# Adaptive-LayerNorm block: the opening's modulation and projections cut by 256 features instead of 512

## The chip, the cores and the metric

The kernel runs on one core of a Trainium2 chip. The metric is the device time of one execution in microseconds (us), taken as the median of several runs. TensorE is called PE in the profile (PEld is its weight load), VectorE DVE, ScalarE ACT, GpSimd POOL, and SyncE, which only issues DMAs here, SP.

## What is computed

The input is x, 2048 tokens of 1024 features, in float32. A conditioning vector c gives six rows of 1024 values, and two sublayers use three rows each:

```python
mod = (silu(c) @ wmod).reshape(1, 6, 1, 1024)        # sa, ca, ga, sb, cb, gb
h = layernorm(x) * (1 + ca) + sa
x = x + ga * attention(h, Wq, Wk, Wv, Wo)            # ga, gb: magnitude at least 0.25
h = layernorm(x) * (1 + cb) + sb
x = x + gb * lora_experts(h, route_w, A, Bw)         # one of 8 experts of rank 16
```

The attention is causal, with 32 query heads and 8 key heads of width 32, and rotates queries and keys by position (cos and sin tables) before the scores.

## The kernel before, in words

The work is one static program: every engine has its queue of instructions in a fixed order, and waits on semaphores. The order has two parts. The function `open_up` (L1334) writes out by hand the *opening*, the projections of token block 0 (256 tokens). From there on, a planner (`plan_order`, L97) searches an order of attention, the other blocks' projections, the output product and the second sublayer; it keeps a list of the eight PSUM banks by the time at which it believes each to be free (`gates`, L1649 to 1655: times on entry are constants), and gives each piece of work the first of them. Its first pieces after the opening are the four flips and the values of block 1, called `second`.

Weights and tokens come through two streams (`Stream`, L579). A stream has a list of wanted loads, taken in order, and `pump` issues as many as there are free buffers: five of 512 KB for weights ("w"), four for tokens ("x"). `free` gives buffers back and pumps again. All these DMAs are issued by SP in program order, so a load whose buffer is still being read holds up what stands behind it on SP. Blocks 0 and 1 share weights that stay on the chip ("resident"): values and keys in `vk` tiles, queries in `wq` tiles.

A `Modulation` item (L762) makes 512 columns of one row of `mod`. It takes four weight tiles, multiplies them with silu(c) (tile `mr`, L790), copies the result to `rows` on DVE (L796), then turns it into columns, one value per partition (tile `mc`, L802), and writes them to `mod_cols[i]` on DVE (L808, L810). Row 1 is the scale, row 0 the shift of the first sublayer. Four items precede everything else, in the order scale, shift (features 0 to 511), scale, shift (features 512 to 1023).

The tokens of a block are normalised in place (L690 to 733, DVE and ACT). A *flip* (`feature_major`, L746) transposes 128 tokens by 512 features on PE into one PSUM bank (`tr_a`, L751) and writes them to `h_t` with scale and shift, four operations of 128 columns: on ACT for the first half of the features (L738), on DVE for the second (L742). `h_t` has eight chunks of 128 features, and each product goes over the chunks: 2 x 8 for values, 2 x 8 for keys (both L684), 4 x 2 x 8 for queries (L975), each of four matmuls on a quarter of the array's columns.

In the opening six banks are held open as sums (0: values, 1: keys, 2 to 5: queries), and banks 6 and 7 alternate for everything else. The order on PE is: items one and two, flips of features 0 to 511, values and keys for these, item three, two query banks, item four, the third query bank, flips of features 512 to 1023, the fourth query bank, then values, keys and the four query banks for the second half. The norm of the second block (`second.pre()`) is issued after the second flips.

Sums leave PSUM at the end: values by a copy on ACT (`keep_values`, L956), keys and queries by `rotary` (L843). It multiplies by cos on DVE into `tcos` (L849), swaps half heads on DVE into `swap` (L850), and on POOL multiplies `swap` by sin (L853) and adds (L854):

```python
tcos = two.tile([P, 2, TB], F32, tag="half", name=f"tcos_{name}", bufs=3)
swap = two.tile([P, 2, TB], F32, tag="half", name=f"swap_{name}", bufs=3)
```

The tag "half" has three buffers, taken in turn by all that use it. The PSUM bank is free after the swap.

Of the kernel before, what the change touches and what calls it, by code (L numbers as in the profile page):

```python
# [10 lines left out]
F32 = mybir.dt.float32  # L11
# [6 lines left out]
P = 128  # L18
T = 2048
D = 1024  # L20
# [5 lines left out]
QB = 512  # L26
NQB = T // QB
TB = 256
# [444 lines left out]
def adaln_block_kernel(  # L473
# [24 lines left out]
    nc = tc.nc  # L498
# [80 lines left out]
    class Stream:  # L579
        def __init__(self, pool, tag, depth):  # L580
            self.pool, self.tag, self.depth = pool, tag, depth
            self.loads, self.tiles = [], []
            self.freed = self.used = 0

        def pump(self, most=1 << 30):
            while len(self.tiles) < min(len(self.loads), self.freed + self.depth, most):
                n = len(self.tiles)
                shape, load = self.loads[n]
                t = self.pool.tile(shape, F32, tag=self.tag, name=f"{self.tag}_{n}")
                load(t)  # L590
                self.tiles.append(t)
# [14 lines left out]
    weights = Stream(wpool, "w", NW)  # L606
    tokens = Stream(xpool, "x", NX)

    def want_wmod(i, half):
        for kp in range(NC // 2):  # L610
            col = i * D + half * 512
            src = wmod[kp * 2 * P : (kp + 1) * 2 * P, col : col + 512].rearrange(
                "(k p) n -> p k n", p=P
            )
            weights.loads.append(([P, 2, 512], lambda t, s=src: nc.sync.dma_start(t, s)))

    resident = {}

    def load_values_keys(kh):

        rows = slice(kh * 512, (kh + 1) * 512)
        t = epool.tile([P, 4, QB], F32, tag="et", name=f"vk_{kh}")
        for i, w in enumerate((wv, wk)):
            nc.sync.dma_start(
                t[:, :, i * TB : (i + 1) * TB], w[rows, :].rearrange("(k p) n -> p k n", p=P)
            )
        resident["vk", kh] = t

    def load_queries(kh, half):
        for kp in (2 * kh, 2 * kh + 1):  # L630
            t = qpool.tile([P, 2, QB], F32, tag="q", name=f"wq_{half}_{kp}")
            nc.sync.dma_start(
                t,
                wq[kp * 2 * P : (kp + 1) * 2 * P, half * 512 : (half + 1) * 512].rearrange(
                    "(k p) n -> p k n", p=P
                ),
            )
            resident["q", half, kp] = t

# [122 lines left out]
    class Modulation:  # L762
# [1 line left out]

        when = -1

        def __init__(self, i, half):
            self.i, self.half = i, half

        def plan(self, push):  # L770
            slow = 0.2 if self.i in mod_cols else 2.4
            return [
                Part(1.7, "C", True, (("dve", 0.7),), chunks=4, push=push),
                Part(0.9, "W", True, (("dve", slow),), frees=4),
            ]

        def want(self):
            want_wmod(self.i, self.half)

        def pre(self):  # L780
            return []

        def main(self, following):
            i, half = self.i, self.half
            parts = weights.take(4)
            ps = bank(f"mr_{i}_{half}")
            for r in range(2):
                for q in range(4):
                    k = r * 4 + q
                    nc.tensor.matmul(  # L790
                        ps[q * HD : (q + 1) * HD, :], silu_p[:, k, :], parts[k // 2][:, k % 2, :],
                        start=(r == 0), stop=(r == 1),
                    )
                weights.free(2)
            rows = two.tile([P, 512], F32, tag="half", bufs=3, name=f"rows_{i}_{half}")
            nc.vector.tensor_copy(rows, ps)  # L796
            following()
            yield 1.7, True
            ps = bank(f"mc_{i}_{half}")
            if i in mod_cols:  # L800
                for j in range(4):
                    nc.tensor.matmul(  # L802
                        ps[:, j : j + 1], rows[:, j * P : (j + 1) * P], ones_p[:, 0:1],
                        start=True, stop=True,
                    )
                dst = mod_cols[i][:, half * 4 : half * 4 + 4]
                if i in (1, 4):
                    nc.vector.tensor_scalar_add(dst, ps[:, 0:4], 1.0)  # L808
                else:
                    nc.vector.tensor_copy(dst, ps[:, 0:4])  # L810
            else:


                nc.tensor.matmul(ps, ones_p, rows, start=True, stop=True)
                cols = slice(half * 512, (half + 1) * 512)
                sgn = two.tile([P, 512], F32, tag="half", bufs=3, name=f"gsgn_{i}_{half}")
# [23 lines left out]
    def sign_rotation(cs):  # L840
        nc.scalar.activation(cs[:, 1, :], cs[:, 1, :], AF.Identity, scale=sign)
# [14 lines left out]
    class Project:  # L856
# [80 lines left out]
        def flip(self, s, kh):  # L937
            feature_major(
                self.h_t[:, :, s * P : (s + 1) * P], self.xt[s], kh, mod_cols[1], mod_cols[0],
                f"a_{self.b}_{s}_{kh}",  # L940
            )

        def first(self, part, k):

# [344 lines left out]
    m = {(i, half): Modulation(i, half) for i in (2, 3, 4, 5) for half in range(2)}  # L1289
# [35 lines left out]
    def fill(n=1):  # L1325
        for _ in range(n + 4):
            step = advance()
            assert step is not None
            n -= bool(step[0])
            if not n:  # L1330
                return step[0]
        raise AssertionError("the next part of an item cannot be issued yet")

    def open_up():  # L1334


# [6 lines left out]
        load_values_keys(0)  # L1343
        load_queries(0, 0)
        fill(2)
        opening.start()
        for s in range(2):
            opening.flip(s, 0)
        chosen[:0] = range(6)
        banks = [bank("open") for i in range(6)]  # L1350

        def values(kh):
            for s in range(2):
                for k in range(4 * kh, 4 * kh + 4):
                    opening.value(banks[0], s, k)

        def keys(kh):
            for a in range(2):
                for k in range(4 * kh, 4 * kh + 4):
                    opening.key(banks[1], a, k)  # L1360

        def queries(kh, i):
            for a in range(2):
                for k in range(4 * kh, 4 * kh + 4):
                    opening.query(banks[2 + i], i // 2, 2 * (i % 2) + a, k)

        values(0)
        keys(0)
        load_queries(0, 1)
        fill(2)  # L1370
        load_values_keys(1)
        for half in range(2):
            load_queries(1, half)
        tokens.pump()
        cs = load_rotation(0, 2)
        for i in range(4):
            opening.query_tiles(i // 2, i % 2)
        queries(0, 0)
        queries(0, 1)
        fill(2)  # L1380
        queries(0, 2)
        for s in range(2):
            opening.flip(s, 1)
            tokens.free()
        sign_rotation(cs)
        for _, act in second.pre():
            act()
        queries(0, 3)
        values(1)
        keys(1)  # L1390
        opening.keep_values(banks[0])
        opening.keep_keys(banks[1])
        for half in range(2):
            for hp in range(2):
                queries(1, 2 * half + hp)
            for hp in range(2):
                opening.keep_queries(banks[2 + 2 * half + hp], half, hp)
        chosen.clear()


# [352 lines left out]
```

## Time and profile before

| | us |
|---|---|
| median of three runs (1755.1 to 1756.59) | 1755.84 |
| the profiled execution | 1754.85 |
| its span, first to last instruction | 1752.6 |
| first matmul | 8.51 |
| first product of the opening | 21.70 |
| end of the opening, first transposes of block 1 | 72.63 |
| first values of block 1 | 74.53 |

The mean granted clock of TensorE is 0.998 of full speed. Over the first 62 us the DMA engines are busy without a break, at 350 to 410 GB/s. In lines of the timeline the first number is the start and the second the length in us, then come engine, line of the kernel, operation and tiles (output<-input); brackets hold the idle time before it and what ended it. Lines of the chain of waits hold start, length and what the chain passed through. Names of tiles are the program's, with buffer numbers left out.

### The profile page before, as it was taken

The numbers are of one execution on the slowest core, as the hardware profiler recorded it, in microseconds if no ns is written. First come the engines' busy times: TensorE is split into PE (matmuls) and PEld (weight loads), VectorE is DVE, ScalarE is ACT, GpSimd is POOL, SyncE is SP. The second block draws the span as 40 slices with busy tenths as digits, with TensorE's granted clock in tenths as the row PEclk, the third lists the DMA queues.
The fourth block names the chain that finished last, engine by engine and source line by source line (L and its number), as shares of the span: only waits on it lengthen the run. The fifth ranks groups of instructions, "written<-read, shape, count | busy, mean of one in ns | idle before, by whom it ended". The sixth has DMA issues, their size and how long they took to land.

```text
span 1752.6 us, 55165 instructions
## 1 busy us (share of the span) xinstructions
PE 1716.0 (98%) x24616; PEld 704.6 (40%) x24616; DVE 1089.0 (62%) x2160; ACT 737.9 (42%) x1634; POOL 1297.5 (74%) x630
## 2 busy tenths in 40 slices
PE   7999999999999999999999999999999999999997
PEld 3655554444444433334444443323323333333334
DVE  2455556756656764675667545756675675776487
ACT  2203423443543433445435444244444544454463
POOL 1235646578878775869786989789889899898952
PEclk9999999999999999999999999999999999999999
DMA  9502323212322512222013011110111111101001
GB/s 354 185 27 83 115 81 104 64 60 98 104 65 65 180 72 82 73 79 68 24 59 128 26 50 49 68 44 36 50 55 46 48 50 50 73 26 50 34 5 50
DMA packets 68493, 130.52 MB, mean 74 GB/s; under 512 B 3744, under 2 KB 20768, under 8 KB 68256
## 3 DMA queue, kind: packets, MB, share of 16 engines
q1 hardware_dynamic: 66928, 125.85, 20.7%
q8 instruction: 193, 3.16, 0.7%
q10 hardware_dynamic: 1328, 1.15, 0.2%
q14 instruction: 44, 0.36, 0.1%
HBM read 118.59 MB, written 8.39 MB: 72 GB/s over the span
## 4 chain that ended last, share of the span: by engine, by line
PE 77%; POOL 15%; DVE 2%; issue 2%; ACT 1%; DMA 1%; SPq 0%; POOLq 0%; ACTq 0%; DVEq 0%
POOL acc L1571 14%; PE sm L1445 13%; PE po L1553 12%; PE sc L1535 11%; PE pq L975 11%; PE pw L684 10%; PE sc L1521 4%; PE pk L684 3%; PE pv L684 2%; PE pd L1580 2%; PE open L975 2%; PE mr L790 1%; PE pf L684 1%; DVE mx L1452 1%; PE pa L684 1%
## 5 line engine op out<-in xcount | busy, mean ns | idle before, releaser
L1452 DVE TENSOR_REDUCE mx<-sm 128x1 f32<-128x512 f32 (+3 forms) x1280 | 686.7, 601 | 400.7 <-PE sm L1445 399.8
L1571 POOL TENSOR_TENSOR acc<-acc,et 128x2048 f32<-128x2048 f32 (+1 forms) x242 | 905.1, 3740 | 28.1 <-ACT et L1543 14.8
L1543 ACT ACTIVATE et<-sc 128x512 f32<-128x512 f32 (+3 forms) x1280 | 575.5, 543 | 662.4 <-PE sc L1535 645.1
L1445 PE MATMUL sm<-k_t,q 32*128 32x512 f32 (+3 forms) x3328 | 335.3, 475 | 3.0 <-ACT rd L1585 3.0
L1553 PE MATMUL po<-et,v_sb 128*32 128x512 f32 (+3 forms) x2560 | 296.6, 539 | 0.6 <-ACT et L1543 0.5
L1535 PE MATMUL sc<-q,k_t 32*128 32x512 f32 (+3 forms) x2560 | 291.0, 533 | 0.0
L684 PE MATMUL pw<-w,q 128*32 128x512 f32 x1920 | 235.5, 597 | 1.4 <-DMA w<-in_wo_dram 1.4
L1445 PEld LDWEIGHTS sm<-k_t,q 32*128 32x128 f32 x3328 | 139.0, 185 | 131.0 <-issue 48.6
L975 PE MATMUL pq<-h_t,w 128*32 128x256 f32 x3072 | 187.9, 382 | 0.0
L1569 POOL TENSOR_TENSOR acc<-et,et 128x2048 f32<-128x2048 f32 (+1 forms) x31 | 132.1, 4262 | 38.6 <-ACT et L1543 24.9
L975 PEld LDWEIGHTS pq<-h_t,w 128*32 128x32 f32 x3072 | 90.6, 110 | 103.8 <-issue 48.7
L1121 POOL TENSOR_TENSOR x<-ag,x 128x512 f32<-128x512 f32 x40 | 64.4, 1611 | 90.2 <-DVE ag L1120 81.5
L1553 PEld LDWEIGHTS po<-et,v_sb 128*32 128x32 f32 x2560 | 61.7, 109 | 166.9 <-issue 137.7
L1535 PEld LDWEIGHTS sc<-q,k_t 32*128 32x128 f32 x2560 | 119.0, 185 | 14.1 <-issue 2.8
L1589 DVE RECIPROCAL rd<-rd 128x128 f32<-128x128 f32 x128 | 113.6, 922 | 17.0 <-ACT rd L1585 16.8
L1521 PE MATMUL sc<-nt,ones_h 32*128 32x512 bf16 (+3 forms) x1280 | 115.2, 351 | 1.8 <-DVE mx L1452 1.0
L1521 PEld LDWEIGHTS <-ones_h 32*128 32x128 bf16 x1280 | 31.2, 91 | 196.7 <-issue 186.9
L684 PEld LDWEIGHTS pw<-w,q 128*32 128x32 f32 x1920 | 51.4, 109 | 139.5 <-issue 116.9
L853 POOL TENSOR_TENSOR swap_q<-swap_q,cs 128x512 f32<-128x512 f32 x32 | 40.7, 1273 | 60.9 <-DVE swap_q L850 60.8
L853 POOL TENSOR_TENSOR swap_k<-swap_k,cs 128x512 f32<-128x512 f32 x8 | 10.2, 1277 | 94.7 <-DVE swap_k L850 94.7
L1120 DVE TENSOR_TENSOR ag<-pw,gate 128x512 f32<-128x512 f32 x40 | 27.5, 686 | 63.4 <-PE pw L684 61.5
L1593 POOL TENSOR_TENSOR q<-q,rd 128x512 f32<-128x512 f32 x31 | 39.6, 1277 | 35.4 <-DVE rd L1589 28.8
(146 smaller groups left out, 1278.4 us busy)
## 6 DMA issues: line engine op xcount, KB each, us to landing
w<-in_wo_dram SPq DMA_DIRECT2D x112, 256.0 KB
w<-in_wmod_dram SPq DMA_DIRECT2D x48, 512.0 KB
w<-in_wq_dram SPq DMA_DIRECT2D x48, 512.0 KB
x<-in_x_dram SPq DMA_DIRECT2D x32, 512.0 KB
out_dram<-x SPq DMA_DIRECT2D x16, 512.0 KB
w<-in_wv_dram SPq DMA_DIRECT2D x12, 512.0 KB
w<-in_wk_dram SPq DMA_DIRECT2D x12, 512.0 KB
wq<-in_wq_dram SPq DMA_DIRECT2D x8, 512.0 KB
```

Source lines behind the costliest of these rows:

```text
L684: nc.tensor.matmul(dst[rows], left[:, rows], right, start=start, stop=stop)
L975: nc.tensor.matmul(ps[j * HD : (j + 1) * HD, a * TB : (a + 1) * TB], self.query_weights(half, k, j * P + h * HD), self.h_t[:, k, :], start ...
L1121: nc.gpsimd.tensor_add(x1[t][:, cols], tmp, x1[t][:, cols])
L1445: nc.tensor.matmul(ps[j][:, a:b], q[rows, t * P : (t + 1) * P], k[rows, kc * QB + o : kc * QB + o + b - a], start=not masked, stop=(t, a, ...
L1452: nc.vector.tensor_reduce(mx[:, t, j : j + 1, kc], ps[j][:, a:b], AX.X, ALU.max)
L1521: nc.tensor.matmul(ps[j][:, a:b], ones_h[rows, :], nt[rows, off:], start=(kc == kcs[0]), stop=False,)
L1535: nc.tensor.matmul(ps[j][:, a:b], k[rows, kc * P : (kc + 1) * P], q[rows, off:], start=False, stop=(kc == kcs[-1]),)
L1543: nc.scalar.activation(self.ets[kc][:, j, off:], ps[j][:, a:b], AF.Exp, scale=1.0 / math.sqrt(HD))
L1553: nc.tensor.matmul(self.po[rows, off:], v_sb[:, kc, 4 * (self.m // 4) + j, :], et[:, j, off:], start=(i == 0), stop=(i == self.nk - 1),)
L1569: self.adder.tensor_add(self.acc[:, :, off:], first[:, :, off:], et[:, :, off:])
L1571: self.adder.tensor_add(self.acc[:, :, off:], self.acc[:, :, off:], et[:, :, off:])
L1589: nc.vector.reciprocal(part, part)
```

## The change

An item of the opening now makes scale and shift of the *same* 256 features, so that after each item two chunks of `h_t` can be made and multiplied. Its four weight tiles are each filled by two DMAs of 256 columns. `flip_chunks` transposes two chunks of both token tiles into one bank and applies scale and shift by two operations of 256 columns, both on ACT. The resident weights are loaded by 256 rows: one call of `load_resident` issues four DMAs (values, keys, two halves of queries). `Stream.pump` keeps its limit, so that SP's order of wmod and resident weights is set by `weights.most`.

The opening is a loop over four steps of 256 features: values, keys, three query banks, half of the fourth, the next item's rows, the other half, the item's columns, the next flips. The last step has no item and keeps each sum as it is done. The norm of the second block comes after the last flips, ahead of the last step. The planner, its constants and what follows the opening are as before.

```diff
@@ Stream @@
-        def pump(self, most=1 << 30):
-            while len(self.tiles) < min(len(self.loads), self.freed + self.depth, most):
+            self.most = 1 << 30
+        def pump(self, most=None):
+            self.most = most or self.most
+            while len(self.tiles) < min(len(self.loads), self.freed + self.depth, self.most):
@@ wanted loads @@
-    def want_wmod(i, half):
...
+    def want_wmod(pieces):
         for kp in range(NC // 2):
+            def load(t, kp=kp):
+                at = 0
+                for i, col, n in pieces:
+                    nc.sync.dma_start(
+                        t[:, :, at : at + n],
+                        wmod[kp * 2 * P : (kp + 1) * 2 * P, i * D + col : i * D + col + n].rearrange(
+                            "(k p) n -> p k n", p=P
+                        ),
+                    )
+                    at += n
+            weights.loads.append(([P, 2, 512], load))
-    def load_values_keys(kh):
-    def load_queries(kh, half):
...
+    def load_resident(kp):
+        rows = slice(kp * 2 * P, (kp + 1) * 2 * P)
+        kh, at = kp // 2, kp % 2 * 2
+        if kp % 2 == 0:
+            resident["vk", kh] = epool.tile([P, 4, QB], F32, tag="et", name=f"vk_{kh}")
         for i, w in enumerate((wv, wk)):
             nc.sync.dma_start(
+                resident["vk", kh][:, at : at + 2, i * TB : (i + 1) * TB],
+                w[rows, :].rearrange("(k p) n -> p k n", p=P),
             )
+        for half in range(2):
             t = qpool.tile([P, 2, QB], F32, tag="q", name=f"wq_{half}_{kp}")
             nc.sync.dma_start(
+                t, wq[rows, half * 512 : (half + 1) * 512].rearrange("(k p) n -> p k n", p=P)
             )
             resident["q", half, kp] = t
@@ Modulation.main @@
+                at = 0
+                for i, col, n in self.pieces:
+                    dst, n = mod_cols[i][:, col // P : (col + n) // P], n // P
+                    if i in (1, 4):
+                        nc.vector.tensor_scalar_add(dst, ps[:, at : at + n], 1.0)
+                    else:
+                        nc.vector.tensor_copy(dst, ps[:, at : at + n])
+                    at += n
@@ Project @@
+        def flip_chunks(self, k0):
+            ps = bank(f"tr_a_{self.b}_{k0}")
+            for i in range(2):
+                for s in range(2):
+                    nc.tensor.transpose(
+                        ps[:, (2 * i + s) * P : (2 * i + s + 1) * P],
+                        self.xt[s][:, (k0 + i) * P : (k0 + i + 1) * P], ident,
+                    )
+            for i in range(2):
+                modulate(
+                    self.h_t[:, k0 + i, :], ps[:, i * TB : (i + 1) * TB],
+                    mod_cols[1], mod_cols[0], k0 + i, True,
+                )
@@ items @@
-    start_items = [Modulation(i, half) for half in range(2) for i in (1, 0)]
+    start_items = [Modulation((1, col, TB), (0, col, TB)) for col in range(0, D, TB)]
@@ open_up @@
         tokens.pump(2)
-        weights.pump()
+        weights.pump(4)
+        load_resident(0)
+        weights.most = 8
         chosen.extend([6, 7] * 8)
         for _, act in opening.pre():
             act()
         fill(2)
...
+        load_resident(1)
         opening.start()
...
+        opening.flip_chunks(0)
         chosen[:0] = range(6)
         banks = [bank("open") for i in range(6)]
...
+        def queries(kp, i, parts=range(2)):
+            for a in parts:
+                for k in (2 * kp, 2 * kp + 1):
+                    opening.query(banks[2 + i], i // 2, 2 * (i % 2) + a, k)
+        for kp in range(4):
+            for s in range(2):
+                for k in (2 * kp, 2 * kp + 1):
+                    opening.value(banks[0], s, k)
+            for a in range(2):
+                for k in (2 * kp, 2 * kp + 1):
+                    opening.key(banks[1], a, k)
+            if kp == 3:
+                opening.keep_values(banks[0])
+                opening.keep_keys(banks[1])
+                for i in range(4):
+                    queries(kp, i)
+                    if i % 2:
+                        for hp in range(2):
+                            opening.keep_queries(banks[1 + i + hp], i // 2, hp)
+                break
+            for i in range(3):
+                queries(kp, i)
+            weights.most = 12 + 4 * kp if kp < 2 else 1 << 30
+            queries(kp, 3, [0])
+            fill(1)
+            if kp == 0:
+                load_resident(2)
+            elif kp == 1:
+                load_resident(3)
+                cs = load_rotation(0, 2)
+                tokens.pump(1 << 30)
+            queries(kp, 3, [1])
+            fill(1)
+            opening.flip_chunks(2 * kp + 2)
+            if kp == 2:
+                tokens.free(2)
+                sign_rotation(cs)
+                for _, act in second.pre():
+                    act()
         chosen.clear()
```

More of the change, by code (lines that the diff above doesn't have):

```diff
@@ L607, in adaln_block_kernel @@
     tokens = Stream(xpool, "x", NX)
-    def want_wmod(i, half):
+    def want_wmod(pieces):
         for kp in range(NC // 2):
[L611 to L615, printed above, removed]
-    resident = {}
-    def load_values_keys(kh):
-        rows = slice(kh * 512, (kh + 1) * 512)
-        t = epool.tile([P, 4, QB], F32, tag="et", name=f"vk_{kh}")
+            def load(t, kp=kp):
[9 more added lines that the diff above has]
+            weights.loads.append(([P, 2, 512], load))
+    resident = {}
+    def load_resident(kp):
[3 more added lines that the diff above has]
+            resident["vk", kh] = epool.tile([P, 4, QB], F32, tag="et", name=f"vk_{kh}")
         for i, w in enumerate((wv, wk)):
             nc.sync.dma_start(
-                t[:, :, i * TB : (i + 1) * TB], w[rows, :].rearrange("(k p) n -> p k n", p=P)
-            )
-        resident["vk", kh] = t
-    def load_queries(kh, half):
-        for kp in (2 * kh, 2 * kh + 1):
+                resident["vk", kh][:, at : at + 2, i * TB : (i + 1) * TB],
+                w[rows, :].rearrange("(k p) n -> p k n", p=P),
+            )
+        for half in range(2):
             t = qpool.tile([P, 2, QB], F32, tag="q", name=f"wq_{half}_{kp}")
             nc.sync.dma_start(
[L633 to L636, printed above, removed]
+                t, wq[rows, half * 512 : (half + 1) * 512].rearrange("(k p) n -> p k n", p=P)
             )
@@ L765, in adaln_block_kernel, with __init__ @@
         when = -1
-        def __init__(self, i, half):
-            self.i, self.half = i, half
+        def __init__(self, *pieces):
+            self.pieces = pieces
         def plan(self, push):
-            slow = 0.2 if self.i in mod_cols else 2.4
+            slow = 0.2 if self.pieces[0][0] in mod_cols else 2.4
             return [
@@ L777, in want @@
         def want(self):
-            want_wmod(self.i, self.half)
+            want_wmod(self.pieces)
         def pre(self):
@@ L783, in main @@
         def main(self, following):
-            i, half = self.i, self.half
+            i, col, _ = self.pieces[0]
             parts = weights.take(4)
-            ps = bank(f"mr_{i}_{half}")
+            ps = bank(f"mr_{i}_{col}")
             for r in range(2):
@@ L794, in main @@
                 weights.free(2)
-            rows = two.tile([P, 512], F32, tag="half", bufs=3, name=f"rows_{i}_{half}")
+            rows = two.tile([P, 512], F32, tag="half", bufs=3, name=f"rows_{i}_{col}")
             nc.vector.tensor_copy(rows, ps)
@@ L798, in main @@
             yield 1.7, True
-            ps = bank(f"mc_{i}_{half}")
+            ps = bank(f"mc_{i}_{col}")
             if i in mod_cols:
@@ L805, in main @@
                     )
[L806 to L810, printed above, removed]
+                at = 0
[6 more added lines that the diff above has]
+                    at += n
             else:
                 nc.tensor.matmul(ps, ones_p, rows, start=True, stop=True)
-                cols = slice(half * 512, (half + 1) * 512)
-                sgn = two.tile([P, 512], F32, tag="half", bufs=3, name=f"gsgn_{i}_{half}")
+                cols = slice(col, col + 512)
+                sgn = two.tile([P, 512], F32, tag="half", bufs=3, name=f"gsgn_{i}_{col}")
                 nc.vector.tensor_scalar(sgn, ps, 0.0, 0.5, ALU.is_ge, ALU.subtract)
@@ L1286, in adaln_block_kernel @@
     opening, second = Project(0), Project(1)
-    start_items = [Modulation(i, half) for half in range(2) for i in (1, 0)]
+    start_items = [Modulation((1, col, TB), (0, col, TB)) for col in range(0, D, TB)]
     early, late = outputs(0)
-    m = {(i, half): Modulation(i, half) for i in (2, 3, 4, 5) for half in range(2)}
+    m = {(i, half): Modulation((i, half * 512, 512)) for i in (2, 3, 4, 5) for half in range(2)}
     phases = [
@@ L1342, in open_up @@
         fill(2)
-        load_values_keys(0)
-        load_queries(0, 0)
-        fill(2)
+        load_resident(1)
         opening.start()
-        for s in range(2):
-            opening.flip(s, 0)
+        opening.flip_chunks(0)
         chosen[:0] = range(6)
         banks = [bank("open") for i in range(6)]
[L1352 to L1375, printed above, removed]
         for i in range(4):
             opening.query_tiles(i // 2, i % 2)
-        queries(0, 0)
@@ L1379, in open_up @@
[L1379 to L1397, printed above, removed]
+        def queries(kp, i, parts=range(2)):
+            for a in parts:
+                for k in (2 * kp, 2 * kp + 1):
+                    opening.query(banks[2 + i], i // 2, 2 * (i % 2) + a, k)
```

## The prediction, on record before the changed kernel ran

> **What bounds the kernel now.** I read the page first, then the chain of waits in order of time over the first 90 us, the timeline of VectorE at the end of the opening, and a table of stretches for DMA rates and the granted clock. The page says that TensorE sets the time:
>
> ```profile
> PE 1716.0 (98%) x24616; PEld 704.6 (40%) x24616; DVE 1089.0 (62%) x2160; ACT 737.9 (42%) x1634; POOL 1297.5 (74%) x630
> ...
> PE 77%; POOL 15%; DVE 2%; issue 2%; ACT 1%; DMA 1%; SPq 0%; POOLq 0%; ACTq 0%; DVEq 0%
> ```
>
> Nothing past the opening is edited. The question is how much sooner or later TensorE comes through the opening and into the second block. The chain there (start, length, what):
>
> ```profile
> 8.51 5.50 PE mr L790 x16
> ...
> 14.04 0.70 DVE rows L796
> ...
> 14.88 1.02 PE mc L802 x8
> ...
> 21.70 7.11 PE open L684 x128
> ...
> 33.13 7.04 PE open L975 x128
> 40.17 1.79 PE mr L790 x16
> ...
> 41.98 0.70 DVE rows L796
> ...
> 42.72 1.05 PE mc L802 x8
> ...
> 72.70 1.90 PE tr_a L751 x16
> 74.60 7.04 PE pv L684 x128
> ```
>
> The chain runs on TensorE from 8.5 us to beyond 88 us, apart from DVE's copies of 0.7 us, so a delay here is paid at the end in full. The products begin at 21.70, the opening ends at 72.63, the second block's values begin at 74.53. The next view is VectorE at that border:
>
> ```profile
> 58.95 0.69 DVE L849 TENSOR_TENSOR tcos_k<-open,cs 128x512 f32<-128x512 f32 x1 [3.33 <-PE open L684]
> ...
> 59.57 0.74 DVE L850 STREAM_SHUFFLE swap_k<-open 128x512 f32<-128x512 f32 x1
> ...
> 66.74 0.01 DVE L850 LOAD_MASK_SELECT swap_q<-open  x1 [0.19 <-POOL q L854]
> ...
> 73.73 0.73 DVE L850 STREAM_SHUFFLE swap_q<-open 128x512 f32<-128x512 f32 x1
> 74.36 2.63 DVE L742 TENSOR_SCALAR h_t<-tr_a,mod,mod 128x128 f32<-128x128 f32 x8
> ```
>
> Five rotations (keys, four query banks) stand one behind the other. From the third on, a shuffle waits for POOL: three "half" buffers serve them, so each shuffle needs the buffer that the rotation before it gives back after its POOL addition. The shuffles start 3.50 us apart (66.74, 70.24, 73.73). Before, that costs nothing, because TensorE finishes a query bank every 3.5 us too. Behind the last shuffle in DVE's queue stand the second block's transposed features (L742), needed at 74.53 + 4 x 0.43 = 76.26, when the values reach feature chunk 4. They come 1.5 us early.
>
> **The change, part by part.**
>
> *The start.* One item instead of two precedes the products. Its four loads now have rows of 1 KB, where they had 2 KB:
>
> ```profile
> 8.00:12.50 4.50, 3.99 (x14) 0.73 (x16) 3.95 (x13) 0.81 (x4) 1.59 (x4) 1.00 1.05 402
> ...
> 36.50:39.50 3.00, 3.00 (x61) 1.82 (x56) 0.00 (x0) 0.00 (x0) 0.00 (x0) 1.00 1.08 352
> 293.39:296.80 3.41, 0.36 (x4) 0.22 (x2) 2.91 (x5) 0.83 (x4) 1.81 (x2) 1.00 0.00 0
> 296.80:300.21 3.41, 3.41 (x13) 0.28 (x13) 0.69 (x1) 2.55 (x11) 1.24 (x1) 0.51 0.00 0
> 300.21:303.63 3.42, 3.42 (x68) 2.02 (x68) 1.11 (x4) 0.00 (x0) 3.34 (x2) 0.50 0.02 5
> 303.63:307.04 3.41, 2.94 (x52) 1.41 (x48) 3.30 (x11) 1.32 (x5) 0.79 (x2) 0.99 0.00 0
> ```
>
> (Columns: stretch, length, busy time of PE, PEld, DVE, ACT and POOL, granted clock, DMA share, GB/s.) The first row moves wmod in 2 KB rows, the second the key and value weights in 1 KB rows: 402 against 352 GB/s. The Trainium skill ("DMA: Bandwidth & Descriptors", Specifications) puts the line rate at 512 B and more; by it the halved rows cost nothing, by the row 2.10 MB take 5.96 instead of 5.22 us. I take the row, +0.7 us. SP issues twice as many descriptor sets, near 0.45 us each, 0.9 us per 512 KB against 1.5 us of transfer: hidden by the transfer. So the item's matmuls end at 14.7, its rows and columns at 15.90 + 0.7 = 16.6.
>
> Then two column writes on DVE (0.16 each, overlapping), beside four transposes (0.55), and one ACT activation of 256 columns: no such row; 128 columns took 0.47, the copy of 512 took 0.56; I take 0.50. With gaps of 0.04 that is 0.9 us, paid again at each later flip. Products start at S = 17.5, 4.2 us sooner than before. x is normalised by 15.3, and the first resident weights lie ahead of the second item's wmod in SP's queue: 1.57 MB after 13.1 us, key and value weights by 14.6, queries by 17.3.
>
> *The steps.* The products are 768 instructions before and after; 128 took 6.93 us (33.06 to 39.99), so a step of 192 takes 10.4 us and all four 41.6. Three items lie between: 1.79 for rows, 0.99 for columns (42.72 to 43.71); the 0.8 us wait for the copy is covered by half a query bank (0.87 us), and costs up to 0.8 each without it. DMA needs per step 2.10 + 0.52 MB at 352 and 1.05 MB at 384, 10.2 us against 14.1 us of TensorE: hidden. In SP's queue, wmod pieces wait for buffers that TensorE frees, and the next resident weights, the rotation tables and x stand behind them; the third item frees its buffers from 41.5 on, then 4.5 + 4.2 + 4.0 us of transfer bring x for the second block by 55, 4 us before use. The last columns are done at t4 = 17.5 + 31.2 + 3 x 2.78 + 2 x 0.9 = 58.9, and the opening ends at 58.9 + 0.9 + 10.4 = 70.2, against 72.63. So the opening alone gains **2.4 us**: the five stalls it loses (second item's DMA, four waits) are partly given back by flips that products no longer cover.
>
> *The end of the opening.* Four steps leave only a quarter of the query products, 6.9 us, behind the keys; before it was 13.9 us. The rotation chain does not shrink with it. The second block's norm, moved here, takes DVE 5.05 us (50.55 to 55.6) from t4 + 0.3 on and stands ahead of the first rotation, so that starts at 64.2 (the keys themselves are ready at 63.2). From it to the last shuffle is 73.73 - 58.95 = 14.78 us, the buffers' pace, hence 79.0; the features behind it start 0.63 later and the first is there 0.44 after that: **80.05 us**. TensorE has its transposes and waits: query banks 3 and 4 are what the second block's fourth flip and its values get (the planner's list of free banks takes 0, 1, 2, 3, then 4), given back at 72.7 and 76.2, then four chunks (1.74 us), then the wait for 80.05. Before, that chunk started at 76.26. **Sum: +3.8 us**, the 2.4 gained included. On ACT the rotation's sign (0.72) and the norm's parts keep their order (the 5.05 us hold them), and the copy of the values waits for the norm, until about 66: no one needs that bank before 70. SP's next two x loads wait for the second block's flips, 3 us later than before; they are used from 125 on.
>
> *The clock.* From 70.2 to 80.05 TensorE has about 4 us of work. In the trace, a stretch of 3.41 us with 0.36 us busy (L1445 waiting for ACT, idle 3.05) was followed by two at half clock, 6.8 us. Counted on in steps of 3.41 us, the emptiest stretch inside the program that was not followed so is 1727.05 to 1730.46, with 1.57 us busy. In the new stall the worst stretch (72 to 76) holds 0.6 to 1.3 us, between the two. The skill ("TensorE: Matmul & The Clock Gate", Part 1) has the clock back after one busy window of about 3.4 us; by that a fall near 75.5 ends by 79 and costs 0, by the row it lasts to 82.3 and costs half of 2.2 us. Bounds 0 and 2.0; no gain is possible in this stall itself. I take the row, 1.0.
>
> Total +4.8 us. The profiled execution took 1754.85 us for a span of 1752.6, and would take 1759.65; it lies 0.99 under the median, 1755.84, so the forecast is 1760.6 us.
>
> **Rivals.**
> - *No new stall* (the features are not held by the rotations, or the norm's delay and the banks bite less): the opening's 2.4 us are kept, 1753.4. The 3.50 us pace speaks against it; it is within the bound below unless the start gains 1.1 us more. Chance 0.08.
> - *Not slower: the half-clock stretch at 296.8 goes.* It exists because an idle time of 3.05 us fell almost wholly into one 3.41 us stretch. A shift of 3.8 to 4.8 us is 1.1 to 1.4 stretches; if the grid stays tied to the start, the idle time is split and neither part is empty enough. [...]Worth 1.5 to at most 3.4 us (half of 6.8): net near +1.9, 1757.7. Against it: the grid may drift from run to run, and three runs within 1.5 us show no such jump. Chance 0.20.
> - *The start is slow too*: between 14.7 and 17.5 TensorE has only columns and transposes; if the clock falls there, the first products lose 1.7 to 3.4 us, and with wmod's 1 KB rows slower than the weights' the time is near 1764. Against it: the stretch 13.5 to 16.9 still holds about 2 us of work. Chance 0.10.
>
> **How the numbers follow.** The forecast case has 0.62, with its own range 1758.8 to 1762. A measurement tells 0.2% (3.5 us) from no change, so slower begins at 1759.35: 0.50 of the forecast case and the slow start's 0.10 make 0.60. Within: 0.12 of the forecast, 0.18 of the lost stretch, 0.05 of the first rival, 0.35. Faster: 0.05, what is left of these two. The range reaches to the lost stretch below and the slow start above: 1757.0 to 1764.0.
>
> **What would show it.** Products begin near 17.5; the opening ends near 70.2; the first rotation starts after the norm, not after the keys; shuffles 3.5 us apart; second block's value chunk 4 at 80, with an idle time of TensorE before it that ends on DVE's L742, and two shorter ones that end on shuffles; half clock near 76 to 82. I am wrong if the rotations run closer together, if the flips get other banks or another place in DVE's queue, or if items two to four wait for wmod.

## The result and the profile after

The changed kernel takes 1760.66 us (median of 10 runs, 1757.83 to 1761.85), the kernel before 1755.47 us beside it (10 runs, 1753.65 to 1758.49). The ratio is 1.0027, with a 95% interval of 1.0018 to 1.0035: slower by 3.2 to 6.1 us. The profiled execution took 1759.55 us for a span of 1757.8, against 1752.6 before.

TensorE works almost as long as before (1717.2 against 1716.0 us), so most of the added time is waiting. The page's chain of waits now runs less on TensorE (71% instead of 77%) and more on POOL, DVE and DMA. These shares don't locate the loss, for 6% of the span is over 100 us: the chain takes other ways later on too, where nothing was edited.

```profile
PE 1717.2 (98%) x24616; PEld 704.9 (40%) x24616; DVE 1086.8 (62%) x2156; ACT 738.6 (42%) x1634; POOL 1297.5 (74%) x630
...
PE 71%; POOL 20%; issue 3%; DVE 3%; DMA 2%; ACT 1%; SPq 0%; POOLq 0%; ACTq 0%; DVEq 0%
```

The chain of waits of the changed kernel in order of time (start, length, what) shows the place:

```profile
17.11 3.68 PE open L692 x64
20.80 6.04 PE open L1001 x112
26.84 1.72 PE mr L798 x16
28.56 0.86 PE open L1001 x16
29.42 1.03 PE mc L810 x8
30.45 0.51 PE tr_a L959 x4
...
30.98 0.57 ACT h_t L746
...
31.60 3.68 PE open L692 x64
...
68.88 0.75 DVE swap_q L861 x2
...
69.70 1.29 POOL swap_q L864
...
71.06 1.29 POOL q L865
...
79.35 0.72 DVE swap_q L861 x2
80.07 0.30 DVE h_t L750
...
80.42 5.39 PE pv L692 x96
```

A step takes 14.49 us (17.11 to 31.60). Before 80 us the chain leaves TensorE: it goes through the rotations on DVE and POOL, and returns only with DVE's first transposed feature (L750, which was L742). (From 60.28 to 66.18 the view names a DMA of x as what the first POOL operation waited for. That operation stands 1.00 us behind its shuffle, and 0.98 before, so the DMA most likely only happened to end at that moment.) The timeline of the border, TensorE and the waits that end on it:

```profile
62.35 1.91 PE L692 MATMUL open<-h_t,vk 128*32 128x256 f32 x32
...
64.46 0.21 DVE L723 TENSOR_SCALAR off_a<-mv_a,rstd_a 128x1 f32<-128x1 f32 x1
64.59 0.68 DVE L860 TENSOR_TENSOR tcos_k<-open,cs 128x512 f32<-128x512 f32 x1
...
71.10 1.53 PE L759 MATMUL tr_a<-ident,x 128*128 128x128 f32 x12
...
73.25 0.63 PE L759 MATMUL tr_a<-ident,x 128*128 128x128 f32 x4 [0.62 <-DVE swap_q L861]
...
76.76 9.05 PE L692 MATMUL pv<-vk,h_t 128*32 128x256 f32 x128 [2.88 <-DVE swap_q L861]
...
79.35 0.01 DVE L861 LOAD_MASK_SELECT swap_q<-open  x1 [2.17 <-POOL q L865]
...
79.97 2.63 DVE L750 TENSOR_SCALAR h_t<-tr_a,mod,mod 128x128 f32<-128x128 f32 x8
```

Four things can be read here. The first rotation follows the norm's last operation (L723) without idle time; but the keys' products end only at 64.26 (62.35 + 1.91), so the norm holds the rotations up by 0.3 us at most. The fourth flip and the values each wait for a shuffle that gives a bank back. The last shuffle waits for POOL. The values take 9.05 us because they stop in their middle for L750. In the kernel before, the values and the keys behind them ran without a stop; the first two lines are of before, the third of the change:

```profile
74.53 7.11 PE L684 MATMUL pv<-vk,h_t 128*32 128x256 f32 x128
81.46 7.09 PE L684 MATMUL pk<-h_t,vk 128*32 128x256 f32 x128
...
85.63 7.09 PE L692 MATMUL pk<-h_t,vk 128*32 128x256 f32 x128
```

The second block's keys start at 85.63 instead of 81.46: **+4.17 us**. The opening had ended at 71.10 instead of 72.63, so 1.5 us were gained and 5.7 lost at the border.

The delay stays at 4.17 us up to 290 us. That the span ends 5.2 us longer has mostly to do with the clock, which the table of stretches shows (columns as in the prediction):

```profile
76.47:79.89 3.42, 3.13 (x32) 1.73 (x32) 1.25 (x4) 0.00 (x0) 2.54 (x2) 0.55 0.41 152
...
301.75:305.17 3.42, 3.42 (x65) 1.79 (x64) 0.69 (x1) 1.76 (x8) 2.04 (x1) 0.55 0.02 5
1731.00:1735.35 4.35, 1.56 (x51) 1.19 (x43) 4.14 (x15) 1.80 (x6) 2.49 (x2) 1.00 0.01 4
1735.35:1738.77 3.42, 3.42 (x65) 2.92 (x59) 1.93 (x7) 1.80 (x4) 0.00 (x0) 0.55 0.01 2
```

The first row's clock of 0.55 means that its edges are a little off: the half clock ran from 76.80 to 80.21, within the wait for L750. The one near 300 lasted 3.4 us here and 6.8 in the profile of before, and behind it the delay is 2.9 us (the same POOL operations compared in both traces). It creeps back to 3.6 by 1700 us; why, was not traced. The half clock at 1735 is new and makes it 5.2. It stands behind an idle time of 2.79 us that before had too (2.78) without a fall. The clock changes of this profile at 76.80, 80.21, 302.08, 305.49 and 1735.68 lie 1, 65, 1 and 419 times 3.413 us apart. Counted in such steps, the idle time at 1735 falls almost wholly into one step here, while in the profile of before a border of two steps (1730.46) cuts it in parts of 1.8 and 0.9 us. So half clocks of this kind come and go between executions.

### The profile page after: what moved, and what is told of

It reads as the page before. It is cut to its first block, busy times and chain, and to the rows that moved or that the text cites. A ratio compares the mean times of both kernels' runs of the same rounds, so it can differ in the third digit from the quotient of the medians.

```text
span 1757.8 us, 55206 instructions
## 1 busy us (share of the span) xinstructions
PE 1717.2 (98%) x24616; PEld 704.9 (40%) x24616; DVE 1086.8 (62%) x2156; ACT 738.6 (42%) x1634; POOL 1297.5 (74%) x630
## 4 chain that ended last, share of the span: by engine, by line
PE 71%; POOL 20%; issue 3%; DVE 3%; DMA 2%; ACT 1%; SPq 0%; POOLq 0%; ACTq 0%; DVEq 0%
POOL acc L1593 17%; PE sm L1467 12%; PE pq L1001 11%; PE po L1575 10%; PE sc L1557 10%; PE pw L692 9%; PE sc L1543 4%; PE pk L692 3%; PE pv L692 2%; PE pd L1602 2%; DVE mx L1474 1%; PE open L1001 1%; PE pf L692 1%; PE pa L692 1%; PE sm L1454 1%
## 5 line engine op out<-in xcount | busy, mean ns | idle before, releaser
L1593 POOL TENSOR_TENSOR acc<-acc,et 128x2048 f32<-128x2048 f32 (+1 forms) x242 | 905.1, 3740 | 26.8 <-ACT et L1565 13.5
```

The source lines that it names most:

```text
L1593: self.adder.tensor_add(self.acc[:, :, off:], self.acc[:, :, off:], et[:, :, off:])
```

## The experiments

The theory after the result is this: TensorE's chain is cut at the border by DVE's in-order queue, where the second block's features stand behind five rotations paced by three buffers; two banks are the next waits under it. The rivals: the banks are the whole wait; POOL itself is the pace; or the opening itself loses (1 KB rows, uncovered flips). Where matmuls are added whose results nobody reads, it is said.

**1. Features of block 1 all from ACT.**

```diff
-            modulate(dst[:, k, :], ps[:, j * P : (j + 1) * P], scale, shift, k, kh == 0)
+            modulate(dst[:, k, :], ps[:, j * P : (j + 1) * P], scale, shift, k, kh == 0 or name.startswith("a_1_"))
```

> The changed kernel, with all of block 1's transposed features written by ACT instead of half of them by DVE behind the rotations. Theory (DVE's queue is the wait that ends last, the PSUM banks are one step ahead of it): the wait for L750 near 80.4 goes, and the next in line is query bank 4, given back near 76.7; block 1's keys then start near 83.7 if the clock stays up (85.4 if it halves from 76.5 on) instead of 85.63, so 0.3 to 2 us faster than the change. Rival (banks are the whole wait): no gain at all. Rival (the loss lies in the opening, in wmod's 1 KB rows and the new flips): no gain, still about 5 us slower than before.

Measured: 1758.49 us (12 runs), ratio to before 1.0021 (1.0013 to 1.0030). The timeline of TensorE:

```profile
72.60 1.53 PE L759 MATMUL tr_a<-ident,x 128*128 128x128 f32 x12
74.76 0.63 PE L759 MATMUL tr_a<-ident,x 128*128 128x128 f32 x4 [0.63 <-DVE swap_q L861]
78.27 8.73 PE L692 MATMUL pv<-vk,h_t 128*32 128x256 f32 x128 [2.89 <-ACT h_t L746]
86.82 3.42 PE L692 MATMUL pk<-h_t,vk 128*32 128x256 f32 x60
```

The stop in the middle of the values is gone, the two bank waits are as they were, and the values still take 8.73 us: now the half clock (78.2 to 81.6 here) falls on work instead of on a wait. (The view names ACT for the 2.89 us. But the values start 0.14 us behind the shuffle that gives their bank back, as they did in the change, 0.15 us, and in run 3 the same work on ACT doesn't hold them: the bank was the wait.) All is 1.5 us later than in the change, because the opening ended at 72.60; why, is the subject of runs 8 to 12. With these 1.5 us the expected 85.4 is 86.9, and 86.82 was measured. The median is 2.2 us below the change's, but the two were not measured beside each other, and the intervals of their ratios overlap: a gain of this edit alone is seen in the trace (0.3 us), not shown in the time.

**2. Other banks.** Flips and values of block 1 get banks that the opening left early; the planner is untouched.

```diff
-        chosen.extend([6, 7] * 8)
+        chosen.extend([2, 3] * 8)
...
-        chosen[:0] = range(6)
+        chosen[:0] = [0, 1, 4, 6, 7, 5]
```

> The changed kernel, with the opening's banks renumbered so that the four flips and the values of block 1 get banks that the opening left early; DVE's order is as in the change. Theory: the two waits for shuffles before the flips and the values go, but the wait for DVE's features near 80.4 stays in full, so block 1's keys still start near 85.6 and the time is that of the change (0 to 1.7 us slower if the idle time, now in one piece, brings the clock down). Rival (banks are the wait): 3 to 4 us faster than the change.

Measured: 1763.02 us (5 runs), ratio 1.0046 (1.0033 to 1.0060). TensorE again:

```profile
72.90 1.97 PE L759 MATMUL tr_a<-ident,x 128*128 128x128 f32 x16
74.80 1.93 PE L692 MATMUL pv<-vk,h_t 128*32 128x256 f32 x32
82.24 6.92 PE L692 MATMUL pv<-vk,h_t 128*32 128x256 f32 x96 [5.51 <-DVE h_t L750]
88.99 1.25 PE L692 MATMUL pk<-h_t,vk 128*32 128x256 f32 x20
```

Transposes and first chunks run without a wait, and the whole wait, 5.51 us in one piece, now ends on L750. It then costs more: the half clock comes at 82.0, on the 96 instructions behind it, which take 6.92 us instead of 5.39. So the banks are not what ends last; in the change they only broke the same wait into pieces. No gain came, let alone the 3 to 4 us of the rival.

**3. Both edits.**

> Both edits: features of block 1 all from ACT, and banks that are free early. Theory: no wait is left at the border; transposes at 71.1, values near 73.0, keys near 80.0 instead of 85.63 (81.46 before): 5.6 us faster than the change and 1.5 us faster than the kernel before, which is what the opening itself gained. Rival (the opening itself loses): no better than the kernel before, or slower.

Measured: 1752.89 us (13 runs), ratio 0.9991 (0.9983 to 0.9999), 1.8 us below the 1754.67 beside it. In its profile TensorE goes from the transposes through the values without a wait (values 74.56, keys 81.49), but both are 1.5 us later than expected, for the reason of run 1. The profiled execution is one of the slower ones (1754.54 us). Together the two edits take away the loss; singly each leaves the other's wait.

**4. Swap buffers of their own** for block 0's rotations, alternating between two tiles that are used only later; the three "half" buffers then serve `tcos` alone.

```diff
-        swap = two.tile([P, 2, TB], F32, tag="half", name=f"swap_{name}", bufs=3)
+        if b == 0:
+            spare = "xn" if name in ("k_0", "q_0_0_1", "q_0_1_1") else "h2"
+            shape = [P, D] if spare == "xn" else [P, NC, P]
+            swap = one.tile(shape, F32, tag=spare, name=f"swap_{name}")
...
+        else:
+            swap = two.tile([P, 2, TB], F32, tag="half", name=f"swap_{name}", bufs=3)
```

> The changed kernel, with two buffers of their own for the swapped halves of block 0's rotations (taken from tiles that are used only later), so that three half buffers serve the rest. Theory (the rotations are paced by their buffers, 3.50 us each): the pace falls to POOL's two operations, 2.7 us, and shuffles run ahead of POOL: the last one starts near 74.3 instead of 79.35, features behind it at 75, block 1's keys near 80.6: 4.5 to 5 us faster than the change, near the kernel before. Rival (POOL itself is the pace): 79 or later, at most 0.5 us gained.

Measured: 1755.78 us (13 runs), ratio 1.0002 (0.9994 to 1.0010). DVE's timeline:

```profile
66.66 0.68 DVE L868 TENSOR_TENSOR tcos_k<-open,cs 128x512 f32<-128x512 f32 x1
...
73.46 0.01 DVE L869 LOAD_MASK_SELECT swap_q<-open  x1 [1.20 <-POOL q L873]
...
76.05 0.01 DVE L869 LOAD_MASK_SELECT swap_q<-open  x1 [1.28 <-POOL q L873]
...
76.69 2.63 DVE L750 TENSOR_SCALAR h_t<-tr_a,mod,mod 128x128 f32<-128x128 f32 x8
```

The shuffles are 2.59 us apart instead of 3.50, which is POOL's two operations, and from the first rotation to the last shuffle it is 9.4 us instead of 14.8. On TensorE the wait for the features is nearly gone:

```profile
77.15 5.39 PE L692 MATMUL pv<-vk,h_t 128*32 128x256 f32 x96 [0.16 <-DVE h_t L750]
82.35 7.09 PE L692 MATMUL pk<-h_t,vk 128*32 128x256 f32 x128
```

Without the 1.5 us of the start the keys would begin at 80.85 (80.6 expected). The median is 1.1 us above the 1754.67 beside it. So the border alone, with TensorE's order and the banks left as they were, gives back most of the difference. That the pace was the buffers' is shown.

**5. Flips covered.** Banks and ACT as in run 3; in each step the item moves half a query bank sooner, and the other half follows the flips.

```diff
-            queries(kp, 3, [0])
             fill(1)
...
-            queries(kp, 3, [1])
+            queries(kp, 3, [0])
             fill(1)
             opening.flip_chunks(2 * kp + 2)
+            queries(kp, 3, [1])
```

> Banks and ACT as in the third run, and in each step the item moved half a query bank sooner, so that half a query bank stands behind the flips' transposes as well and covers the columns' way through DVE and ACT. Theory: each of three flips loses its wait of about 0.6 us (transposes end, activation 0.57, gaps), so the opening ends near 69.2 and block 1's keys start near 78.1: 1.5 to 2 us faster than the third run, 3 to 3.5 us faster than the kernel before. Rival (the copy of the rows or the next item's loads become the wait): as the third run or slower.

Measured: 1752.42 us (21 runs), ratio 0.9983 (0.9976 to 0.9989), 2.4 us below the 1754.85 beside it. The keys start at 80.14, 1.35 sooner than in run 3, with a half clock at the start in both profiles. The median is only 0.65 us further below its own kernel before than run 3's, where 1.5 to 2 were expected: a miss, and within the spread, so that a gain over run 3 is seen in the trace alone.

**6. The idle time filled** with 28 matmuls that nobody reads, at the end of the changed opening.

```diff
+        ps = bank("busy")
+        for _ in range(7):
+            by_columns(
+                ps[:, :TB], opening.h_t[:, 7, :P], opening.value_weights(7), start=True, stop=True
+            )
         chosen.clear()
```

> The changed kernel, with 28 matmuls that nobody reads (about 3 us of TensorE) put at the end of the opening, where TensorE would only wait; the output is the same. Tests the term for the clock. If the half-clock stretch from 76.5 to 79.9 costs nothing, because it lies within the wait for DVE (theory now, after the profile): the stretch goes, block 1's keys still start near 85.6, and the time stays within 1 us of the change. If it costs (the forecast's term): about 1 us faster. If these matmuls delay the flips beyond the wait: slower by up to 1 us.

Measured: 1761.18 us (5 runs), ratio 1.0033 (1.0020 to 1.0046). No half clock is left between 75 and 80 us (granted clock 1.00 there, 0.68 in the change), and the time doesn't fall. The keys start at 87.18, 1.5 later than expected, once more by the start, and no sooner for the better clock. So in the change the half clock at 76 costs nothing by the trace; the times alone, with these intervals, could not tell 1 us.

**7. The kernel before with the edits of run 3.**

> The kernel before, with the same two edits as the third run (block 1's features all from ACT, banks renumbered). Theory: nothing there was waited for, since the rotations kept pace with the query banks; no change, within 1 us. Rival (these edits are worth something by themselves): faster than the kernel before by more than 1 us, and the gain of the third run isn't the opening's.

Measured: 1755.32 us (13 runs), ratio 1.0002 (0.9994 to 1.0011). Where the rotations keep pace with the query banks, neither edit is worth anything.

**The start.** Runs 1 to 6 all showed what the profile of the change did not: a half clock at 16 to 21 us, just as the first products begin. It takes about 1.5 us. Runs 8 to 12 look for the reason.

**8. Run 5 with seven bf16 matmuls that nobody reads** in the waits behind the first item.

```diff
-        fill(2)
+        fill(1)
+        chosen.insert(0, 5)
+        ps = bank("busy")
+        def busy(n):
+            for _ in range(n):
+                nc.tensor.matmul(
+                    ps, ones_h, pick.rearrange("p a n -> p (a n)"), start=True, stop=True
+                )
+        busy(4)
+        fill(1)
         load_resident(1)
         opening.start()
         opening.flip_chunks(0)
+        busy(3)
```

> The fifth run with seven bf16 matmuls of 512 columns that nobody reads, four in the wait for the copy of the first item's rows and three in the wait for the first features; the output is the same. Theory (columns and transposes don't count as work for the clock, so the stretch between the first item's rows and the first products is nearly empty, and the clock halves at about 17 us): the half-clock stretch near 16 to 21 us is gone, the products of the first step take 1.7 us less than in the fifth run, block 1's keys start near 78.4 instead of 80.1, and the time falls by 1 to 1.7 us. Rival (it is the phase of the clock's grid alone, or the weight of work elsewhere): the half-clock stretch stays, no gain.

Measured: 1750.60 us (11 runs), ratio 0.9975 (0.9966 to 0.9984), 4.2 us below the 1754.83 beside it; the keys start at 77.66 and there is no half clock before 293 us. It is faster than both kernels and has the lowest ratio of all, though its interval overlaps run 5's. The keys are 2.5 us sooner than in run 5. The added matmuls can have brought only 1.6 of these: the first item's matmuls ended at 14.11 instead of 14.96, before the first added one, and so the first product began at 17.10 instead of 18.02.

**9. The change with these seven matmuls**, and **10. the change again**, on the same chip.

> The changed kernel with the same seven idle matmuls at its start, nothing else. If the start's half clock is part of what the change usually costs: block 1's keys start near 85.6 as in the profile of the change that had no half clock there, where the first, second and sixth run had 86.8 to 87.2 or more with it, and the median is 1 to 1.7 us below the change's 1760.66. Rival: as the change, within 0.5 us.

> The changed kernel once more, on the chip of these two runs, for a second profile. If the start's half clock is usual and the first profile was the exception: a half-clock stretch near 17 us and block 1's keys near 87 instead of 85.63. If it is rare: the first profile's course again.

Measured: 1759.58 us (7 runs) with them, ratio 1.0028 (1.0017 to 1.0038), 1759.13 us (9 runs) without, ratio 1.0030 (1.0020 to 1.0040). The first profile has its keys at 85.44, as expected; but the second has no half clock at the start either, and keys at 85.72. The medians don't differ the way I expected: a miss. In the change itself the price of the start is not shown.

**11. Run 3 with the seven matmuls**, and **12. run 3 again**, on one chip.

> The third run's kernel (banks renumbered, block 1's features from ACT) with the seven matmuls at the start that nobody reads; beside the third run's kernel itself, on the same chip. Theory (in most executions the clock halves behind the first item): no half-clock stretch before 290 us, block 1's keys near 79.9, and 1 to 1.7 us faster than the kernel beside it. Rival (the start's half clock is no part of the usual time): within 0.5 us of it.

> The third run's kernel again, as the pair of the eleventh on one chip: 1.5 to 2 us faster than the kernel before, as it was; a half-clock stretch near 17 us in its profile if that is usual (six of eight profiles with this start had one).

Measured: 1752.80 us (14 runs), ratio 0.9983 (0.9975 to 0.9991), and 1754.29 us (13 runs), ratio 0.9994 (0.9986 to 1.0002). The pair is 1.5 us apart, as expected. The intervals of their ratios to the kernel before overlap, but the two can be compared with each other, on one chip: resampled from the recorded times, the difference of the medians has a 95% interval of 0.3 to 2.5 us. The granted clock of each run fits: 0.998 is the middle of run 11's and 0.997 of run 12's, and one stretch of 3.41 us at half clock is worth 0.001 of the span. (In runs 9 and 10 both middles are 0.997.) Run 12 lies 1.35 us below its kernel before, where 1.5 to 2 were expected, and its interval takes in no difference: the gain of run 3 over the change is firm, that over the kernel before is not. The profile of run 12 happens to have no half clock at the start; keys at 80.21, and 79.71 in run 11. The table of stretches of run 3, where it had one:

```profile
13.50:17.00 3.50, 2.26 (x16) 1.31 (x12) 0.92 (x3) 1.73 (x3) 0.00 (x0) 0.97 1.06 379
17.10:20.50 3.40, 3.21 (x36) 1.50 (x40) 0.00 (x0) 0.59 (x2) 0.00 (x0) 0.55 1.10 348
```

and of run 11:

```profile
13.50:17.00 3.50, 3.49 (x25) 1.99 (x27) 0.92 (x3) 1.73 (x3) 0.00 (x0) 1.00 1.06 377
17.10:20.50 3.40, 3.40 (x68) 1.95 (x64) 0.00 (x0) 0.20 (x1) 0.00 (x0) 1.00 1.10 348
```

In 3.4 us the one gets through 36 matmul instructions, the other through 68. Of nine profiles with this start, six had the half clock; of three with the added matmuls none. The six have the clock up first at 13.3 to 14.4 us, the other three (the change, runs 10 and 12) at 11.9 to 12.4. Steps of 3.41 us from there put most of the quiet time between the item's last matmul and the first product (14.1 to 17.1 us in the change) into one step in the six, and cut it in two, at 15.4 to 15.8, in the three. That is consistent with the steps' phase deciding; no run set it. It is not the phase alone: run 8 has its clock up at 13.28, as run 6 has at 13.32, and only run 6, without the added matmuls, falls.

## Why the prediction was right, point by point

- **The mechanism was right, step by step.** The first rotation starts behind the norm (forecast 64.2, measured 64.59), the last shuffle at 79.35 (79.0), values chunk 4 at 80.42 (80.05), the waits for banks at 73.25 and 76.76 (72.7 and 76.2). Runs 1 to 4 show each link: DVE's features last, banks under them, buffers as the pace. One link weighs less than was thought: the keys were forecast ready at 63.2, 1.0 us ahead of the norm's end, and were ready at 64.26, so that the norm cost 0.3 us. With the opening later than forecast (next point), keys and norm were done at nearly the same time.
- **The opening's gain was forecast too large**, 2.4 for 1.5 measured. Two terms of the step were too small: the copy of the rows was covered but for 0.16 us (28.38 + 0.86 to 29.40), and columns plus flip took 2.20 us (29.40 to 31.60) instead of 0.99 + 0.9; the activation in it, taken as 0.50, took 0.57. With 0.07 less for the rows that is 0.4 a step, 1.2 in three.
- **The start was 0.4 us better than forecast** (17.11 for 17.5). The last wmod piece came 0.5 us later than before, at 12.88 (0.7 was taken from the 1 KB row's rate), and its matmuls took 1.07 us, as the clock was up already. Between 8 and 12 us the DMAs move 357 GB/s, against 403 before: the measured row was nearer than the 512 B of the Trainium skill ("DMA: Bandwidth & Descriptors", Specifications), by which nothing was to change.
- So the sum at the border, forecast +3.8, measured +4.17.
- **The clock's term of 1.0 us was wrong in its place.** I let the half clock last 6.8 us after the row at 296.8, and so cost 1.0 beyond the wait. It lasted 3.41 us, and ended at 80.21, before chunk 4 (80.42): cost 0, and the trace of run 6 agrees. The Trainium skill ("TensorE: Matmul & The Clock Gate", Part 1), clock back after one busy window, was nearer here than the row, which had a stretch of few matmuls behind it (13 instructions in 3.41 us).
- **The rival "the start is slow too" was set aside on a false reason**: that the stretch 13.5 to 16.9 holds about 2 us of work. It does, by the profile (2.26 us busy in run 3), and the clock fell nevertheless in six of nine profiles. I gave it 0.10. Run 11 against run 12 shows 1.5 us for it on run 3's kernel; what it adds to the change's own median is open, for runs 9 and 10 don't show it.
- **The rival "the half-clock stretch at 296.8 goes"** happened by half in the profile of the change (3.4 us instead of 6.8), and a new one came at 1735. From +4.17 at 86 us the change is +5.2 at its end; single executions of one kernel differ by 4 to 5 us, so that this 1.0 tells nothing of the mean.
- The forecast, 1760.6, lies on the median. That closeness is in part luck: the border was forecast 0.4 short, the clock's 1.0 stood in the wrong place, and 0.4 us lay between the two medians of the kernel before. The border's 4.17 is the part that the runs explain; the other 1 us between the medians is not tied to any one half clock.

## What to carry to other kernels

When a reordering makes the last part of a stage shorter, look at the chains that ran hidden beside that part: here rotations of 3.5 us each, as long as the products of a query bank that covered them, with the next stage's input behind them in the same queue. Such a chain is found before the change by its pace and by what its steps wait for (a buffer, not an engine), and in the reordered kernel two small edits at the border (run 3) or two more buffers (run 4) were worth more than the 1.5 us that the reordering gained; in the kernel before, the edits of run 3 were worth nothing (run 7). A wait with several links under it gives nothing when only a lower link is removed (run 2), and one link is worth only the distance to the next (run 1, by its trace).

## What the runs showed of the hardware

Busy time in the profile is not what keeps TensorE's clock up. In the six falls at the start, the 3.41 us before the fall held 1.89 to 2.41 us of one-column products, transposes and the item's last matmuls; in the kernel before, a stretch with 1.57 us (1727.05 to 1730.46) was not followed by half clock. With 1.85 us of dense matmuls in the waits (1.04 + 0.81 us) none of three profiles fell. Which of the small operations count for less, the one-column products or the transposes, no run separates. An idle time of 2.88 us behind 0.63 us of transposes (the change) and one of 5.51 us (run 2) both brought half clock for 3.41 us; what it cost, 0 or 1.5 us, depended on whether a wait or work lay behind it.
